# First attention input loaded in both orders, its statistics spread by products of ones with diagonals, keys and queries in one pass

## The chip, the core and the metric

The kernel runs on one core of one Trainium2 chip. The metric is device time of one execution in microseconds (us). Engine names are those of the profile: PE (TensorE matmul), PEld (its weight load), DVE (VectorE), ACT (ScalarE), POOL (GpSimd), SP (SyncE, which issues the DMAs).

## The reference, cut to what matters

Two sequences of 1024 tokens with 1024 features go through attention A (32 heads, rotary positions, causal, with ten adapter rows), a mixture feed-forward, attention B, and the feed-forward again, each behind a layernorm and with a residual. Only the entrance of stage A matters here, and only for the first sequence:

```
def _layernorm(x, axis=-1, eps=1e-05):
    m = jnp.mean(x, axis=axis, keepdims=True)
    v = jnp.var(x, axis=axis, keepdims=True)
    return (x - m) / jnp.sqrt(v + eps)
...
qkv = jnp.einsum('btc,oc->bto', x, w_attn)        # x is the normalized input
q, k, v = jnp.split(qkv, 3, axis=-1)
q = _apply_rope(q, cos, sin)
k = _apply_rope(k, cos, sin)
...
ak, av = (adapter rows through the k and v parts of w_attn)
```

All tensors are fp32. The tensor engine contracts over partitions, so the products for q, k and v need the normalized x with features on partitions (xnT), while x as it lies in memory has tokens on partitions, where mean and deviation of a token are found.

## The kernel before, in words

Tokens come in 8 tiles of 128 (t = 0 to 7), features in 8 blocks of 128 (c), tokens also in two halves of 512 (n). Heads are made in groups of four (g = 0 to 7): one group's keys and queries are 128 rows each, a group of values is made two at a time. The attention of group 0 starts as soon as its first half is there, and runs while later groups are projected.

*Order.* The order on PE, POOL and SP is that of the program text. On DVE and ACT a scheduler orders the instructions when the kernel is built; the built order is fixed, and each engine takes its instructions in that order. The projections are Python generators that a `Filler` steps between the rounds of the attention (`attend`, L478), by a budget of estimated nanoseconds; its `chores` (L64 to L70) are small DVE, POOL or DMA steps, one issued at each step of the generators, and `flush` issues what is left of one kind.

*Entrance before (L1089 to L1105).* SP loads four x tiles (`x_load`, tag "pr"), the adapter rows adT, the key and query weights of group 0 (`qk_load`), the value weights (`v_load`), then four further x tiles among cos, sin and gate. `layernorm` (L242) does for each tile two bn_stats and one bn_aggr on DVE (L247, L251), a few 128x1 operations on DVE and ACT (L254 to L267), and the normalization of 128x1024 on DVE (L271). `half` (L758) turns four tiles by PE transposes (`transposed`, L285, 32 of 128x128 for a half), whose banks DVE and ACT copy in turn into xnT (L233, L235). The first half is turned before the projection, the second (passed as `between`) inside it.

*First projection (`project_first`, L958).* For each half: eight k products of 512 columns (kp), then eight q products (qp), one bank each, then the values (`values_first`, L1044, vp, four tiles of 128 tokens). `rotate` (L915) applies the rotary positions to a finished bank: DVE shuffles (L920) and multiplies by cos (L921), POOL multiplies by sin and adds (L924, L925). Between k and q of the first half stands `adapter_keys` (L902): a small product akp and the DVE product aks (L905). `adapter_parts` (L892) makes the adapter rows' keys (ap_k) and values (ap_v, L897), `adapter_values` (L908) makes avp on PE and avs on DVE (L912). Between the halves stand `between`, then `begin(0, 1)`, which makes ap_k of group 1, and `combine(0)`, which queues chores.

*Banks.* PSUM has one bank under the tag "ps" (`bank`, L161), used in turn by ownT, ap_k, akp, ap_v, the adapter scores (as), avp and the next ap_k; a pair ca, cb (`next_bank`, L167) for the projections; two double banks for the scores sc; and one for y. A product into a bank waits until the last reader of what was there is done.

*Splitting.* `mm` (L196) issues a product either whole or as four products of 32 columns of the weights; `flip`, a transpose, switches to whole, the attention's rounds switch to split.

*SBUF.* The "tt" ring has five 128x512 buffers; "mo" two of 128x1024; "h16" two, which hold xnT of the two halves.

Of the kernel before, what the change touches and what calls it, by code (L numbers as in the profile page):

```python
# [14 lines left out]
F32 = mybir.dt.float32  # L15
# [133 lines left out]
def tile_model(ctx: ExitStack, tc: tile.TileContext, d, out: bass.AP):  # L149
# [17 lines left out]
    def next_bank(shape, name):  # L167
        pair.rotate(1)
        return block_bank(shape, name, 1)
# [424 lines left out]
    def stage_a(wk, big):  # L594
        ca = wk
        identb = of["identb"] = ca.tile([P, P], BF16, tag="identb", name="identb", bufs=1)
        dve.tensor_copy(identb, ident)
# [27 lines left out]
        dve.tensor_reduce(tosum[:, 0, :], ones_at, AX.X, ALU.add)  # L625
        for h in range(1, 4):
            pool.tensor_copy(tosum[:, h, :], tosum[:, 0, :])
# [130 lines left out]
        def half(b, n, xns):  # L758

            xnT[b, n] = big.tile([P, NC, HF], F32, tag="h16", name=f"xnT{b}_{n}")  # L760
            for i in range(4):
                yield from transposed(xns[4 * n + i], xnT[b, n][:, :, i * P : (i + 1) * P], f"a{b}_{4 * n + i}", by=(next_bank, next_bank))

        def moments_ahead():
# [26 lines left out]
            def load(c):  # L791
                for k in (c, c + 4):
                    x = big.tile([P, T], F32, tag="t4k", name=f"xc{k}")
                    sp.dma_start(x, d["x1T"][k * P : (k + 1) * P, :])
                    at.append(x)
# [139 lines left out]
        def project(b, g, between=None):  # L935
# [9 lines left out]
            if b == g == 0:  # L945
                yield from project_first(between)
            else:
                yield from project_blocks(b, g)
# [9 lines left out]
        def project_first(between):  # L958
            wqk = wqk_at[0, 0]
            yield adapter_parts("k0", lambda c: wqk[:, c, 1, :], P)  # L960
            for n in range(2):
                if n == 1:
                    yield from between
                    yield from begin(0, 1)
                    combine(0)
                xh = xnT[0, n]
                for s, key in ((1, "k"), (0, "q")):
                    qp = next_bank([P, HF], f"{key}p0_{n}")
                    for c in range(NC):
                        mm(qp, lhsT=wqk[:, c, s, :], rhs=xh[:, c, :], start=(c == 0), stop=(c == NC - 1))  # L970
                        yield HF * COL
                    rotate(0, 0, key, n, qp)
                    if n == 0 and key == "k":
                        yield adapter_keys(0)
                yield ("qk", 0, 0, n)
                yield from values_first(n)
            combine_first(0)
# [66 lines left out]
        def values_first(n):  # L1044
# [5 lines left out]
            for t in range(0, 4, 2):  # L1050
# [7 lines left out]
                if n == 0 and t == 2:  # L1058
                    yield adapter_values(0)
            if n == 1:  # L1060
                wv_at[0, 2] = v_load(0, 2)
# [29 lines left out]
        wqk_at[0, 0] = qk_load(0, 0)  # L1091
        wv_at[0, 0] = v_load(0, 0)
        xns = []
        for t in range(NT):
            if t + 4 < NT:
                xs.append(x_load(0, t + 4, wk, "pr"))
            xns.append(layernorm(big if t < 3 else wk, "t4k" if t < 3 else "pt", xs[t], f"a0_{t}"))
            if t == 0:
                sp.dma_start(cos, d["cos"])
                sp.dma_start(sin, d["sin"])  # L1100
                sp.dma_start(gate, d["gating"].partition_broadcast(P))
                tp = bank([NH, P], "ownT")
                flip(tp, own.rearrange("p h j -> p (h j)"), ident)
                dve.tensor_copy(ownT, tp)
        fill.add(half(0, 0, xns))  # L1105
        ahead = moments_ahead()
        for b in range(B):
            for g in range(NG):

                old = b * NG + g - 3  # L1110
                fill.add(project(b, g, half(0, 1, xns) if b == g == 0 else None),
# [715 lines left out]
```

## Time and profile before

| | |
|---|---|
| median of 3 runs | 2320.02 us (2316.45 to 2323.06) |
| the profiled execution | 2318.73 us |
| its span, first to last instruction | 2316.9 us |
| mean granted PE clock | 0.996 |
| PE busy | 2272.1 us, 98% |
| DVE, ACT, POOL busy | 62%, 47%, 26% |
| k products of the first half start | 19.44 us |
| first scores (sc) start | 38.67 us |
| k products of the second half start | 57.81 us |

The profile shows one execution. The chain of waits follows the work that ended last back from the end: at each step to what released it, or to the instruction before it on its engine; its start times differ by some hundredths from those of the timeline, because it counts from the release. The timeline merges like instructions that follow each other: start, length, engine, line, operation, output and inputs, count, and in brackets the idle time before them with what ended it. Stages give each engine's busy time, the granted clock and the DMA's share and rate in a stretch of the span. A fp32 product of 512 columns is two PE instructions, each 592 ns long and 430 ns after the one before it.

### The profile page before, as it was taken

The page shows a single profiled execution, that of the slowest core. Times are in us where ns is not written, and L with a number is a line of the kernel's source. Part 1 is how long each engine was busy: PE and PEld are TensorE (multiplying, and loading weights), DVE is VectorE, ACT ScalarE, POOL GpSimd, SP SyncE. Part 2 cuts the span into 40 slices and gives each one's busy share as a digit, 9 for nine tenths or more (in the row PEclk, how much of TensorE's full clock was granted, in tenths as well). Part 3 has the DMA queues.
Part 4 walks back from the last instruction along what each step waited for, and adds up shares of the span by engine and source line. Part 5 has one row for each costly group of instructions (what it writes and reads, how often), then busy time and mean ns, then how long its engine had stood idle before and what let it go on. Part 6 is the DMA issues. An engine that isn't in the chain of part 4 may idle for free.

```text
span 2316.9 us, 61351 instructions
## 1 busy us (share of the span) xinstructions
PE 2272.1 (98%) x25246; PEld 1039.5 (45%) x25246; DVE 1445.3 (62%) x4394; ACT 1087.4 (47%) x2084; POOL 613.7 (26%) x957
## 2 busy tenths in 40 slices
PE   8999999999999999999999999999999999999999
PEld 4425443454444544345433445575433553233454
DVE  6686677776656666666752246567766765675453
ACT  3356665666656666566652001012455546665100
POOL 1432234343322223222212124202111111122422
PEclk9999999999999999999999999999999999999999
DMA  5443434644433333333322674542323202323553
GB/s 177 157 131 101 126 108 141 195 128 153 150 95 106 94 112 92 102 105 95 109 71 91 207 245 160 163 156 77 114 93 104 99 18 84 110 83 119 181 161 122
DMA packets 188473, 285.78 MB, mean 123 GB/s; under 512 B 20112, under 2 KB 85792, under 8 KB 188192
## 3 DMA queue, kind: packets, MB, share of 16 engines
q1 hardware_dynamic: 188192, 281.86, 37.9%
q8 instruction: 198, 3.24, 0.6%
q14 instruction: 83, 0.68, 0.1%
HBM read 223.58 MB, written 55.58 MB: 120 GB/s over the span
## 4 chain that ended last, share of the span: by engine, by line
PE 88%; DVE 7%; DMA 2%; ACT 1%; issue 1%; POOL 0%; SPq 0%; DVEq 0%; POOLq 0%; ACTq 0%
PE st L415 10%; PE sc L343 7%; PE y L201 6%; PE y_A L437 6%; PE y_f L199 5%; PE x L201 4%; PE z L201 4%; PE z_f L199 4%; PE st L413 3%; PE y_v L201 3%; PE x_f L199 3%; PE y_B L437 2%; PE y_f L201 2%; PE y_p L199 2%; PE z_v L201 2%; PE hp_f L199 2%
## 5 line engine op out<-in xcount | busy, mean ns | idle before, releaser
L549 ACT ACTIVATE pt<-st 128x1024 f32<-128x1024 f32 (+1 forms) x418 | 423.9, 1019 | 541.4 <-PE st L415 422.3
L364 ACT ACTIVATE pr_A<-pr_A,nmax_A 128x896 f32<-128x896 f32 (+7 forms) x512 | 390.1, 766 | 54.2 <-DVE nmax_A L356 53.4
L356 DVE CUSTOM_DVE_ANT_0 pr_A<-sc,mask 128x512 f32<-128x512 f32 (+3 forms) x512 | 250.0, 535 | 173.1 <-PE st L415 88.6
L343 PE MATMUL sc<-kT,qT 32*128 32x512 f32 (+3 forms) x1536 | 317.2, 522 | 3.4 <-POOL qT L925 2.1
L415 PE MATMUL st<-qT,kT 32*128 32x512 f32 (+3 forms) x1536 | 296.2, 486 | 0.0
L356 DVE CUSTOM_DVE_ANT_0 pr_A<-sc,mask,part_A 128x512 f32<-128x512 f32 (+1 forms) x256 | 156.2, 647 | 123.7 <-PE sc L343 76.3
L422 POOL TENSOR_SCALAR_AFFINE_SELECT pt<-pt 128x256 f32<-128x256 f32 x256 | 102.5, 418 | 429.5 <-ACT pt L549 427.1
L240 POOL TENSOR_TENSOR xf<-xf,b_base 128x256 f32<-128x256 f32 x100 | 75.2, 782 | 406.8 <-DVE xn_f L271 283.4
L364 ACT ACTIVATE pr_B<-pr_B,nmax_B 128x1024 f32<-128x1024 f32 x128 | 145.5, 1141 | 33.0 <-DVE nmax_B L356 32.9
L437 PE MATMUL y_A<-pt,v 128*32 128x512 f32 (+3 forms) x1536 | 157.5, 496 | 0.0
L343 PE MATMUL sc<-kq,qk 32*128 32x512 f32 x512 | 135.8, 650 | 3.4 <-DVE nmax_B L356 2.4
L415 PE MATMUL st<-rows_B,kq 32*128 32x512 f32 x512 | 135.9, 647 | 1.2 <-ACT pt L549 1.0
L415 PEld LDWEIGHTS st<-qT,kT 32*128 32x128 f32 x1536 | 129.0, 185 | 14.9 <-issue 10.7
L413 PE MATMUL st<-rows_A,ones 3*128 3x512 bf16 (+3 forms) x768 | 123.2, 329 | 6.4 <-DVE nmax_A L356 4.1
L356 DVE CUSTOM_DVE_ANT_0 pr_B<-sc,zeros,part_B 128x512 f32<-128x512 f32 x128 | 91.0, 747 | 54.6 <-PE sc L343 54.5
L413 PEld LDWEIGHTS <-ones 3*128 3x128 bf16 x768 | 36.2, 91 | 190.0 <-issue 184.0
L924 POOL TENSOR_TENSOR qr<-qr,sin 128x256 f32<-128x256 f32 x64 | 61.6, 962 | 206.7 <-DVE qr L920 201.3
L201 PE MATMUL y<-tt,wqk 128*32 128x512 f32 x960 | 116.1, 594 | 0.0
L356 DVE CUSTOM_DVE_ANT_0 pr_B<-sc,zeros 128x512 f32<-128x512 f32 x128 | 83.5, 686 | 51.7 <-PE sc L343 51.6
L343 PEld LDWEIGHTS sc<-kT,qT 32*128 32x128 f32 x1536 | 109.4, 183 | 11.8 <-POOL qT L925 3.2
L201 PE MATMUL x<-xnT,wqk 128*32 128x512 f32 x936 | 114.0, 600 | 0.0
L364 ACT ACTIVATION_READ_ACCUMULATOR pr_A<-pr_A,nmax_A 128x1 f32 x512 | 97.2, 190 | 0.0
(406 smaller groups left out, 4072.3 us busy)
## 6 DMA issues: line engine op xcount, KB each, us to landing
tt<-td SPq DMA_DIRECT2D x264, 256.0 KB
qkb_f<-tf SPq DMA_DIRECT2D x96, 256.0 KB
qkb_s<-tf SPq DMA_DIRECT2D x84, 256.0 KB
wqk<-in_w_attnT SPq DMA_DIRECT2D x32, 512.0 KB
xf<-x SPq DMA_DIRECT2D x25, 512.0 KB
xa<-in_x SPq DMA_DIRECT2D x16, 512.0 KB
wv<-in_w_attnT SPq DMA_DIRECT2D x8, 1024.0 KB
yd<-ys SPq DMA_DIRECT2D x32, 256.0 KB
```

Of the source, the lines that this page charges most:

```text
L199: return pe.matmul(out, lhsT=lhsT, rhs=rhs, start=start, stop=stop, skip_group_check=True)
L201: pe.matmul(out[i : i + 32], lhsT=lhsT[:, i : i + 32], rhs=rhs, start=start, stop=stop, skip_group_check=True)
L240: pool.tensor_add(dst[:, i : i + 2 * P], a[:, i : i + 2 * P], b[:, i : i + 2 * P])
L343: yield w * COL, lambda: pe.matmul(dst[:, o : o + w], lhsT=self.qt[rows, qc : qc + P], rhs=self.kt[rows, c0 : c0 + w], start=True, stop=True)
L356: minimum[0] = dve.tensor_tensor_reduce(pr[:, c0 : c0 + w], sc[:, i, o : o + w], m, -self.scale, BIG if c0 == 0 else self.part[:, col], AL ...
L364: tc.keep_in_program_order(act.activation(pr[:, :nk], pr[:, :nk], AF.Exp, bias=self.nmax[:, col], scale=-1.0, accum_out=self.sums[:, col]))
L413: yield w * COL / 4, lambda: pe.matmul(dst[:, o : o + w], lhsT=of["ones"][three, :], rhs=self.rows[three, off : off + w], start=True, stop ...
L415: yield w * COL, lambda: pe.matmul(dst[:, o : o + w], lhsT=self.kt[rows, kb * P : (kb + 1) * P], rhs=rhs, start=self.extra, stop=True)
L422: pool.affine_select(out=dg, in_=dg, compare_op=ALU.is_ge, fill=0.0, base=0, pattern=[[0, 2], [1, P]], channel_multiplier=-1)
L437: pe.matmul(self.y[32 * h : 32 * h + 32, off : off + w], lhsT=self.value(h, kb), rhs=pt[h // 2][:, h % 2, o : o + w], start=self.opens, st ...
L549: act.activation(pt[:, :, low_:wide_], st[:, :, low_:wide_], AF.Exp, scale=ts[0][0].scale)
L924: pool.tensor_mul(qr[:, hs], qr[:, hs], sin[:, cols][:, hs])
```

## The change

The host passes the first input also with axes exchanged (xT, for both sequences; before, only the second sequence had it, as x1T). The kernel then loads xT of sequence 0 straight into xnT, in four DMAs of 1 MB, and normalizes it in place. `half` and with it all 64 transposes and their 16 copies go, and so does the 128x1024 normalization of each tile.

Mean and deviation are needed along the columns, in every partition. `moments_first` makes the statistics of four tiles (x tiles are still loaded for that) and two 128x512 tiles that hold, for each of four token tiles, a diagonal of the means or of the reciprocal deviations. `spread_first` multiplies these by a matrix of ones on PE, four products of 128 columns for each, and ACT copies the bank into a `spread` tile. `normalize_first` subtracts and multiplies block by block: eight subtractions and five multiplications on DVE, three multiplications on POOL in two pieces each.

For the first half all of this stands ahead of the projection. For the second half the statistics are issued after the first half's normalization; the spreads are issued on PE inside the first half's values, and the normalization becomes chores under the key "xn".

In `project_first` the first half's k and q products alternate block by block, into two banks; `adapter_keys` comes after both. In the second half k comes before q, as before. SP loads xT, cos and sin ahead of the value weights, and the four later x tiles after those. Some small steps (identb, tosum, ownT) move behind the first half.

```diff
-        def half(b, n, xns):
-            xnT[b, n] = big.tile([P, NC, HF], F32, tag="h16", name=f"xnT{b}_{n}")
+        def moments_first(n, xs):
+            mv = wk.tile([P, 4, 2], F32, tag="mv0", name=f"mv0_{n}", bufs=1)
             for i in range(4):
-                yield from transposed(xns[4 * n + i], xnT[b, n][:, :, i * P : (i + 1) * P], ...)
+                stats = wk.tile([P, 2, 6], F32, tag="stats", name=f"stats0_{4 * n + i}", bufs=2)
+                for h in range(2):
+                    dve.bn_stats(stats[:, h, :], xs[i][:, h * HF : (h + 1) * HF])
+                dve.bn_aggr(mv[:, i], stats)
+            ve, r, e = (wk.tile([P, 4], F32, tag=tag, name=f"{tag}_{n}", bufs=1) for tag in ("ve0", "rs0", "es0"))
+            dve.tensor_scalar(ve, mv[:, :, 1], EPS, None, ALU.add)
+            act.activation(e, ve, AF.Ln)
+            act.activation(r, e, AF.Exp, scale=-0.5)
+            dve.tensor_mul(e, r, r)
+            dve.tensor_mul(e, e, ve)
+            dve.tensor_scalar(e, e, -0.5, 1.5, ALU.mult, ALU.add)
+            dve.tensor_mul(r, r, e)
+            diagonals = []
+            for i, column in enumerate((mv[:, :, 0], r)):
+                dg = big.tile([P, 4, P], F32, tag="tt", name=f"dg{i}_{n}")
+                dve.tensor_mul(dg, ident[:, None, :].to_broadcast([P, 4, P]), column[:, :, None].to_broadcast([P, 4, P]))
+                diagonals.append(dg)
+            return diagonals
+        def spread_first(n, diagonals):
+            for i, dg in enumerate(diagonals):
+                pb = next_bank([P, 4, P], f"spread{i}_{n}")
+                for t in range(4):
+                    mm(pb[:, t, :], lhsT=all_ones[:, :P], rhs=dg[:, t, :], start=True, stop=True)
+                act.copy(spread[i][:, n * HF : (n + 1) * HF], pb.rearrange("p t c -> p (t c)"))
+        def normalize_first(n):
+            cols = slice(n * HF, (n + 1) * HF)
+            for c in range(NC):
+                x = xnT[0, n][:, c, :]
+                yield lambda x=x: dve.tensor_sub(x, x, spread[0][:, cols])
+                if c % 2 and c > 1:
+                    yield lambda x=x: in_pieces(pool.tensor_mul)(x, x, spread[1][:, cols])
+                else:
+                    yield lambda x=x: dve.tensor_mul(x, x, spread[1][:, cols])
...
                 if n == 1:
-                    yield from between
                     yield from begin(0, 1)
+                    fill.flush("xn")
                     combine(0)
                 xh = xnT[0, n]
-                for s, key in ((1, "k"), (0, "q")):
-                    qp = next_bank([P, HF], f"{key}p0_{n}")
-                    for c in range(NC):
-                        mm(qp, lhsT=wqk[:, c, s, :], rhs=xh[:, c, :], start=(c == 0), stop=(c == NC - 1))
-                        yield HF * COL
-                    rotate(0, 0, key, n, qp)
-                    if n == 0 and key == "k":
-                        yield adapter_keys(0)
+                steps = [(key, s, c) for c in range(NC) for s, key in ((1, "k"), (0, "q"))]
+                if n:
+                    steps.sort(key=lambda step: -step[1])
+                qp = {}
+                for key, s, c in steps:
+                    if c == 0:
+                        qp[key] = next_bank([P, HF], f"{key}p0_{n}")
+                    mm(qp[key], lhsT=wqk[:, c, s, :], rhs=xh[:, c, :], start=(c == 0), stop=(c == NC - 1))
+                    yield HF * COL
+                    if c == NC - 1:
+                        rotate(0, 0, key, n, qp[key])
+                if n == 0:
+                    yield adapter_keys(0)
...
                 if n == 0 and t == 2:
                     yield adapter_values(0)
+                if n == t == 0:
+                    spread_first(1, diagonals)
+                    yield 8 * P * COL
+                    for op in normalize_first(1):
+                        fill.chore("xn", op)
...
         wqk_at[0, 0] = qk_load(0, 0)
+        for n in range(2):
+            xnT[0, n] = big.tile([P, NC, HF], F32, tag="h16", name=f"xnT0_{n}")
+        def xt_load(n):
+            for i in range(2):
+                sp.dma_start(xnT[0, n][:, 4 * i : 4 * i + 4, :],
+                             d["xT"][0, 4 * i * P : (4 * i + 4) * P, n * HF : (n + 1) * HF].rearrange("(c p) t -> p c t", p=P))
+        xt_load(0)
+        sp.dma_start(cos, d["cos"])
+        sp.dma_start(sin, d["sin"])
         wv_at[0, 0] = v_load(0, 0)
-        xns = []
-        for t in range(NT):
-            if t + 4 < NT:
-                xs.append(x_load(0, t + 4, wk, "pr"))
-            xns.append(layernorm(big if t < 3 else wk, "t4k" if t < 3 else "pt", xs[t], f"a0_{t}"))
...
-        fill.add(half(0, 0, xns))
+        sp.dma_start(gate, d["gating"].partition_broadcast(P))
+        later = [x_load(0, t, wk, "pr") for t in range(4, NT)]
+        xt_load(1)
+        all_ones = big.tile([P, HF], F32, tag="tt", name="all_ones")
+        pool.memset(all_ones, 1.0)
+        spread = [big.tile([P, T], F32, tag="mo", name=f"spread{i}") for i in range(2)]
+        spread_first(0, moments_first(0, xs))
+        for op in normalize_first(0):
+            op()
+        diagonals = moments_first(1, later)
+        dve.tensor_copy(identb, ident)
+        dve.tensor_reduce(tosum[:, 0, :], ones_at, AX.X, ALU.add)
...
+        tp = bank([NH, P], "ownT")
+        flip(tp, own.rearrange("p h j -> p (h j)"), ident)
+        dve.tensor_copy(ownT, tp)
...
-        "x1T": a[A + "x"][1].T,
+        "xT": np.swapaxes(a[A + "x"], 1, 2),
```

In the built program of the changed kernel the scheduler put, on DVE, the first three pairs of bn_stats of the second half's tiles ahead of the k shuffle, the fourth pair and the mean diagonal between the k shuffle and aks, and avs behind the whole second normalization and three of the steps that `begin(0, 1)` and `combine(0)` queue (s, tn, s).

## The prediction

> **What bounds the kernel now.** I read the page first, then the chain of waits over the first 150 us, then the timeline, the stages and single tiles there.
>
> ```profile
> PE 2272.1 (98%) x25246; PEld 1039.5 (45%) x25246; DVE 1445.3 (62%) x4394; ACT 1087.4 (47%) x2084; POOL 613.7 (26%) x957
> PE   8999999999999999999999999999999999999999
> ```
>
> TensorE (PE) is busy for 98% of the span; only the first slice stands out. So a microsecond taken from PE's work or its idle time in the opening is a microsecond of the kernel, and one added there is never won back, because what follows has no slack. By the order of the built program, the changed kernel issues on PE exactly the same sequence from the scores that follow the values of the second half on; all differences lie in the first 77 us of the trace of before. The chain there:
>
> ```profile
> 14.09 0.83 DVE xn_a L271
> 15.05 1.94 PE xt_a L205 x8
> ...
> 19.51 7.06 PE kp L199 x16
> 26.72 6.94 PE qp L199 x16
> 33.66 1.00 PE ap_v L897 x16
> 34.66 4.08 PE vp L199 x18
> 38.74 1.08 PE sc L343 x16
> ...
> 51.41 0.56 PE avp L910 x2
> 51.96 0.60 PE xt_a L205 x4
> ...
> 57.30 0.57 PE ap_k L897 x16
> 57.88 7.06 PE kp L199 x16
> ```
>
> (Columns: start, length, what.) From 19.51 on it is PE all the way: keys, queries, adapter values (ap_v), values (vp), first scores (sc), and from 51.96 to 57.30 the transposes of the second half, 5.3 us in which PE mostly waits for copies.
>
> **Step 1, the first products.** Now kp starts at 19.51, behind eight normalized-and-transposed pieces. In the changed kernel DVE makes four statistics without the 0.8 us normalizations (L271): a pair of bn_stats is 1.29, with its bn_aggr a pitch of 1.45, so from 4.59 (first x landed), with the two small copies moved in between, the fourth ends at 10.7. Mean diagonal (no row; the nearest is a 128x512 subtraction, L225, 0.69; bounds 0.64 of L921 and 1.10 of L228 beside POOL) ends at 11.6; four small operations and the second diagonal at 13.1. Each spread is four products, that is 8 PE instructions; 8 transposes took 1.94 at this point, so PE ends at 13.5 and 15.5; ScalarE copies at 0.59 (L235) end at 14.2 and 16.2. The ownT copy stands before the subtractions on DVE and ends at 16.2. Two subtractions and a multiplication at 0.65 give column block 0 at 18.1. Gain **1.4**; if the diagonals or spreads take their bounds, 0.2 to 2.5.
>
> Is xT there? Up to its first half 4.33 MB, to its second 5.38 MB must land. The stages of before moved 1.06, 2.61, 4.20 and 6.17 MB up to 5, 10, 15 and 20 us, so they land at about 15.3 and 18.0; wanted at 16.2 and 20.7. At the slowest full stage (311 GB/s) it is 18.9 for the second: still in time. The 4.2 MB more of DMA are hidden here; the four later x tiles end at 9.57 MB, 29.6 us (32.4 at 311 GB/s), when the statistics that want them wait for PE anyway. DVE's 13 and POOL's 3 normalizing steps run ahead of PE (1.76 per block of k and q).
>
> **Step 2, the cold clock.**
>
> ```profile
> L205 PE MATMUL xt_a<-ident,xn_a x32: 421/421/473, 9.5 to 18.5; 128*128 128x128 f32 x32
> ```
> ```profile
> L205 PE MATMUL xt_a<-ident,xn_a x32: 272/273/331, 51.9 to 57.0; 128*128 128x128 f32 x32
> ```
> ```profile
> 128.00:130.00 2.00, 1.02 (x16) 0.31 (x8) 1.97 (x5) 0.00 (x0) 1.85 (x3) 1.00 0.80 232
> 130.00:131.00 1.00, 0.00 (x0) 0.00 (x0) 0.47 (x1) 0.00 (x0) 0.99 (x1) 1.00 1.16 340
> 131.00:132.00 1.00, 0.89 (x8) 0.31 (x8) 0.00 (x0) 0.00 (x0) 0.92 (x3) 0.77 1.13 273
> 132.00:133.00 1.00, 1.00 (x8) 0.20 (x8) 0.58 (x5) 0.25 (x1) 1.00 (x2) 0.50 0.20 47
> ```
>
> The same transpose takes 421 ns before 18.9 us and 273 later: PE starts slow, and four solid microseconds of transposes ended that just ahead of kp (592 ns each from its first). The second pair of rows (busy PE, PEld, DVE, ACT, POOL; clock; DMA) shows the way back: PE did little from 128.3 to 131.1 and then had a clock of 0.50, for 3.4 us by the stages after it, costing half of that, 1.7. In the changed kernel only spreads, ownT and ap_k, with gaps, run ahead of kp, so I let kp run cold for 3.4 us: **+1.7**, bounds 0 and 3.4.
>
> The Trainium skill, TensorE: Matmul & The Clock Gate, "Part 4: PE-mode transpose", says that transposes do not count as busy and never release the clock. The trace differs: after nothing but transposes kp ran at full rate. By the page, before would have started kp cold too, step 2 would be 0 and the sum 1.7 smaller; I follow the rows.
>
> **Step 3, first new wait.** Now the key bank is finished 7 us before the query bank, and its rotation and the small aks product (L905) hide under qp. Made together, both end together, 14.0 us after the start; the last k product 0.9 earlier. PE's next instruction but one, ap_v (L897), writes the one "ps" bank that aks is read from: it must wait for DVE's aks. And on DVE, in the built order, stand between the wait for kp and aks:
>
> ```profile
> 26.62 0.73 DVE L920 STREAM_SHUFFLE kr<-kp 128x512 f32<-128x512 f32 x1
> ...
> 29.70 0.64 DVE L921 TENSOR_TENSOR kT<-kp,cos 128x512 f32<-128x512 f32 x1
> ...
> 30.37 0.19 DVE L905 TENSOR_TENSOR aks<-akp,own 128x40 f32<-128x40 f32 x1
> ```
>
> shuffle 0.73, bn_aggr 0.20, two bn_stats 1.29 (the eighth tile, stuck behind the shuffle although its data is there), kT 0.65, bn_aggr 0.20, q shuffle 0.73, ve 0.15, diagonal 0.69, es 0.26, qT 0.67, es 0.20, aks 0.19: 5.96; neighbours overlap by some 0.05, so 5.4. That is 4.6 after the end of qp. PE then does ap_v 1.00 and vp 4.08 and reaches the scores 9.7 after qp; before it was 38.74 - 33.66 = 5.1. **+4.6** (bounds 3.8; 5.6 if two of these take 1.10 beside POOL). POOL's rotation ends some 2.5 earlier than sc needs it, so it is not late next; parts_v, one bn_stats and all first softmax rows queue behind, and shift with it.
>
> PE stands 4.3 us, longer than at 128, so the clock falls: 1.7 if it is cold for 3.4 from the restart, up to 3.4 if for two such stretches. **+2.3**, bounds 0 and 3.4.
>
> **Step 4, second new wait.** Take S for the start of sc (38.74 now). ap_k of the second half starts at S+18.56 now. Without transposes PE goes: sc 1.08, 40 vp 2.30, as 0.30, 16 vp 0.86, first spread 0.86 (8 x 0.107), S+5.4. The second spread wants the bank that ACT's copy of v frees; that copy ended at 44.93 now, S+6.2, behind eight exponentials. Then 0.86, sc 1.07, 128 vp 7.05 (120 took 6.61), avp 0.56: S+15.8, 2.8 earlier than now. But ap_k takes the "ps" bank that avs (L912) reads on DVE, and DVE meets avs only behind the whole second normalization: from the first spread copy, S+6.85, 13 steps of 0.65 (8.45), four 512-wide row minima at 0.62 to 0.69 (2.6), two transposes 0.50, s, tn and s at 0.69 (2.07), avs 0.60: 14.2, S+21.1. In before avs ran at 52.0 on an idle DVE. POOL multiplies three blocks at the same time, and DVE steps beside POOL took 1.10 in places: bounds 14.2 and 20 (all 13 steps); I add 0.5. So ap_k at S+21.6, **+3.0** against S+18.56 (bounds 2.5 and 8). PE stands 5.8 us; cold clock again **+2.3** (0 to 3.4). The normalization itself is then done, and kp runs through; in the tile-split form 8 products still take 6.9 (x, L201: 16 in 1.72, two products).
>
> **Sum**: -1.4 + 1.7 + 4.6 + 2.3 + 3.0 + 2.3 = **+12.5 us**. The profiled execution took 2318.73 (span 2316.9 and 1.8 around it); it is 1.3 below the median 2320.02, well inside the runs shown. Forecast 2331.2.
>
> **Rivals.**
> (a) *The clock does not follow.* Only the waits count: -1.4 + 4.6 + 3.0 = +6.2, 2325. For it: PE has scattered work near each wait. Against it: rows 130 to 133. Chance 0.12.
> (b) *The waits stay covered* (not slower). If aks and avs come before PE wants them, there remain the start, -1.4, and the transposes, 15.8 against 18.56, -2.8: -4.2, 2314.5, and 2312 with the start at its better bound and the second spread not waiting for v. It decides where DVE has aks within 0.3 us of the end of qp and avs by S+15.8: DVE would have to be 4.3 and 5.8 us shorter, which no row gives. Against it also is that DVE takes its instructions as they stand in all these rows. Chance 0.11, half of it beyond 0.3%.
> (c) *DVE slower than sized*: most of the 13 steps beside POOL at 1.10 and both cold stretches double: 5 + 2.2 more, 2339 and beyond. Chance 0.05.
>
> The forecast, 0.72, spans 2325 (all lesser bounds) to 2339. 0.3% is 7 us, about what a measurement of this kernel can tell from no change. Beyond +7 lie 0.66 of the forecast, 0.04 of (a), all of (c): 0.75 slower. Within: 0.06, 0.08 and 0.05: 0.19. Faster: 0.06. The range leaves out (b) and most of (c): 2320 to 2340.
>
> **What would show it.** kp starts near 18 and is slow at first; after akp PE idles some 4 us, released by DVE's aks; after avp it idles 5 to 6, released by avs; the granted clock is 0.5 after each; the k products of half two start near 68 instead of 57.9. I am wrong if PE runs through either place, if the clock stays at 1.00, or if something behind 130 us gives time back, which the unchanged PE order speaks against.

## The result, and the profile after

The changed kernel took 2335.31 us (median of 4 runs, 2334.21 to 2339.84) against 2320.68 us of the kernel before beside it (4 runs, 2316.45 to 2323.06): ratio 1.0072, 95% interval 1.0057 to 1.0087. It is slower by 14.6 us; the forecast was 12.5 us slower. The profiled execution took 2334.21 us, 15.5 more than that of before.

The page of the changed kernel, to be held against the two lines shown of before:

```profile
PE 2268.8 (97%) x25424; PEld 1032.8 (44%) x25424; DVE 1453.9 (62%) x4386; ACT 1082.9 (46%) x2068; POOL 629.6 (27%) x970
PE   6899999999999999999999999999999999999999
```

PE has 3.3 us *less* to do (2268.8 against 2272.1), and the span is 15.6 longer: the loss is idle time, and it shows in the first two of the 40 slices, which fell from 8 to 6 and from 9 to 8 tenths. The chain of waits there:

```profile
33.96 0.72 DVE kr L952 x2
...
34.77 1.15 DVE stats L760 x2
...
37.41 0.59 DVE dg L773
...
39.40 0.12 DVE aks L937
...
39.56 1.94 PE ap_v L929 x16
41.50 4.82 PE vp L199 x18
46.32 1.09 PE sc L343 x16
...
61.76 0.57 PE avp L942 x2
62.33 7.17 issue
69.50 1.08 PE ap_k L929 x16
70.58 8.47 PE kp L201 x64
```

In before this stretch was PE from 19.51 on. Now the chain leaves PE twice. From 33.96 to 39.52 it runs over DVE: the rotation of k, statistics of the eighth tile (L760), a diagonal (L773), aks; only then ap_v goes. From 62.33 to 69.50 the chain says "issue": it saw no releaser, but avs (L944) ends at 69.4 on DVE. The stages give a clock of 0.50 from 19.1 to 22.5, from 39.6 to 43.0 and from 66.9 to 73.7 us (1.00 between), so ap_v takes 1.94 (1.00 before), vp 4.82 (4.08), kp 8.47 (7.06).

The scores of the second half start 14.1 us later than before (90.60 against 76.49 by the timeline). The first of ACT's large exponentials (L549) starts at 97.3 us in before and 14.14 us later here; the shift stays within 0.04 of that up to 383 us, but for one exponential (13.87, at 161). Beyond, it moves between 14.0 and 18.0, and the span ends 15.6 later.

### The profile page after: what moved, and what is told of

Read it like the earlier page. It is cut to its first block, busy times and chain, and to the rows that moved or that the text cites. A ratio compares the mean times of both kernels' runs of the same rounds, so it can differ in the third digit from the quotient of the medians.

```text
span 2332.5 us, 61703 instructions
## 1 busy us (share of the span) xinstructions
PE 2268.8 (97%) x25424; PEld 1032.8 (44%) x25424; DVE 1453.9 (62%) x4386; ACT 1082.9 (46%) x2068; POOL 629.6 (27%) x970
## 4 chain that ended last, share of the span: by engine, by line
PE 86%; DVE 7%; DMA 2%; issue 2%; ACT 1%; POOL 0%; SPq 0%; DVEq 0%; POOLq 0%; ACTq 0%
PE st L415 9%; PE sc L343 7%; PE y L201 6%; PE y_A L437 6%; PE y_f L199 5%; PE x L201 4%; PE z L201 4%; PE z_f L199 4%; PE st L413 3%; PE y_v L201 3%; PE x_f L199 3%; PE y_B L437 2%; PE y_f L201 2%; PE y_p L199 2%; PE z_v L201 2%; PE hp_f L199 2%
## 5 line engine op out<-in xcount | busy, mean ns | idle before, releaser
L549 ACT ACTIVATE pt<-st 128x1024 f32<-128x1024 f32 (+1 forms) x418 | 423.4, 1018 | 542.7 <-PE st L415 425.9
L201 PE MATMUL y<-tt,wqk 128*32 128x512 f32 x960 | 116.3, 594 | 0.2
L201 PE MATMUL x<-xnT,wqk 128*32 128x512 f32 x936 | 113.7, 599 | 0.0
```

Of the source, the lines that this page charges most:

```text
L201: pe.matmul(out[i : i + 32], lhsT=lhsT[:, i : i + 32], rhs=rhs, start=start, stop=stop, skip_group_check=True)
L549: act.activation(pt[:, :, low_:wide_], st[:, :, low_:wide_], AF.Exp, scale=ts[0][0].scale)
```

## Experiments

What a whole run shows is uncertain by some us; the trace shows to hundredths where the loss arises, though in one execution. So the table gives for each kernel, from the timeline, the starts of ap_v, of the second half's keys and of its scores (where these stop in between, their second part too), and the **shift**: how much later than in before the first L549 starts. The whole times stand behind. Up to 0.9 us of a shift is no effect of an edit: in the kernels with the changed entrance the first spread starts between 11.37 and 12.29 us, although nothing ahead of it was edited, because the x tiles land at different times (DVE waits 0 to 0.64 us for the third).

| kernel | ap_v | keys 2 | scores 2 | shift | median us (runs) | ratio to before (95%) |
|---|---|---|---|---|---|---|
| before | 33.59 | 57.81 | 76.49 | 0 | | |
| the change | 39.56 | 70.32 | 90.60 | +14.14 | 2335.31 (4) | 1.0072 (1.0057 to 1.0087) |
| e1_keys_early | 36.35 | 68.36 | 88.07 | +11.59 | 2330.24 (7) | 1.0039 (1.0020 to 1.0058) |
| e2_avs_early | 39.12 | 62.56 | 83.32 | +6.88 | 2328.29 (9) | 1.0035 (1.0022 to 1.0049) |
| e3_both_early | 35.26 | 60.47 | 79.07, 82.39 | +7.11 | 2326.43 (10) | 1.0029 (1.0015 to 1.0042) |
| e4_warm | 39.47 | 68.23 | 86.85, 89.30 | +14.02 | 2340.46 (4) | 1.0088 (1.0061 to 1.0115) |
| e5_all_dve | 37.31 | 65.27 | 85.03 | +8.58 | 2324.03 (1) | |
| e6_together_alone | 33.00 | 57.89 | 76.57 | +0.08 | 2320.83 (10) | 1.0005 (0.9995 to 1.0015) |
| e7_other_bank | 35.77 | 59.88 | 78.48, 82.29 | +5.37 | 2323.75 (10) | 1.0010 (1.0001 to 1.0019) |
| e8_all_early | 33.25 | 55.38 | 73.98 | -2.51 | 2317.00 (12) | 0.9981 (0.9972 to 0.9991) |
| e9_second_half | 35.84 | 58.59 | 81.05, 82.14 | +5.22 | 2326.24 (12) | 1.0019 (1.0008 to 1.0031) |
| e10_best | 41.44 | 62.59 | 81.19 | +4.70 | 2324.52 (12) | 1.0025 (1.0012 to 1.0038) |
| e11_late_spread | 32.49 | 55.70 | 74.29, 77.63 | +3.66 | 2322.99 (1) | |
| e12_own_bank | 31.28 | 55.86 | 74.46 | -2.03 | 2316.39 (12) | 0.9992 (0.9980 to 1.0003) |

### Are the two waits what the forecast said they are?

**e1_keys_early** moves akp and aks ahead of the fifth pair of products:

```diff
+                    if n == 0 and (key, c) == ("q", 3):
+                        yield adapter_keys(0)
-                if n == 0:
-                    yield adapter_keys(0)
```

> The changed kernel, but the adapter's keys (akp and aks) are yielded after the query's product of c=3 instead of after the whole loop, so that aks stands on DVE ahead of the rotations and of the eighth tile's moments. Theory (a wait on the bank that aks releases): the 4.65 us in which PE stands before ap_v go, and with them the slow stretch at 39.6 to 43.0; the first scores start at about 41.0 to 42.0 us instead of 46.3 (the second half of qT leaves POOL at 42.8 and then binds). The wait before the second ap_k, for avs behind the second normalization, stays at 5 to 8 us, so the second half's scores start at 84 to 87 us instead of 90.7. Rival (the wait is for something else, the rotations on POOL or the statistics): ap_v still starts at about 39.5 and nothing moves. Time: 2329 to 2332 by the theory, 2335 by the rival.

The 4.65 us went; ap_v followed qp at once. But only 2.55 us of shift were gained. One loss lies ahead of the place of the move: here the start ran at full clock, and the product of c = 3 stood 1.86 us for POOL's xnT. It started 7.28 us after the first kp, exactly as in the change (there slow products had filled the time, and 0.17 was left to wait); but the clock then fell to 0.50, from 26.2 to 29.6. The other loss came up behind the wait removed: PE stood 0.79 us for kT and 1.43 before the second part of the first scores:

```profile
25.44 1.34 PE L199 MATMUL kp<-xnT,wqk 128*128 128x512 f32 x2 [1.86 <-POOL xnT L221]
...
44.52 0.93 PE L343 MATMUL sc<-kT,qT 32*128 32x384 f32 x8 [1.43 <-POOL qT L957]
```

The theory of the wait holds; my price for what is next was too low by some 3 us (the last part of the scores starts at 44.5, where I had expected the first at 41 to 42). The second wait stayed at 7.18.

**e2_avs_early** moves avp and avs ahead of the second spread:

```diff
-                if n == 0 and t == 2:
-                    yield adapter_values(0)
                 if n == t == 0:
+                    yield adapter_values(0)
                     spread_first(1, diagonals)
```

> The changed kernel, but the adapter's values (avp and avs) are yielded at the first v tile of the first half instead of at the third, ahead of the second half's spread and normalization on DVE. Theory (the second ap_k waits for the bank that avs releases, behind the second normalization): PE's 7.2 us before the second ap_k go, and the slow stretch from 66.9 to 73.7 with them; keys of the second half start at 62.5 to 64 us instead of 70.6 and the second half's scores at 81 to 84 instead of 90.7. The first wait (4.65 us) stays. Rival (the normalization itself is what the keys wait for, so that avs only stands at its end by chance): the idle time moves to the second half's kp and stays over 4 us in sum. Time: 2326 to 2329 by the theory, 2331 to 2335 by the rival.

As the theory said: ap_k ran at 62.12, keys at 62.56, scores at 83.32. Stops of 1.14 us (ACT's copy of the spread) and 1.96 (xnT from POOL, c = 3) took the place of 7.2, 3.1 in sum, less than the rival's 4.

**e3_both_early** makes both edits.

> The changed kernel with both moves of the two experiments above: adapter's keys after the query's c=3, adapter's values at the first v tile. Theory: both waits go and both slow stretches; keys of the second half at 57 to 60 us (before 57.9, after 70.6), the second half's scores at 76 to 79 (before 76.6, after 90.7). The two waits with the cold stretches are then the whole loss, and the earlier start of the products is worth about 1 us: 2318 to 2323. Rival (the change costs besides, by 13 slower steps on DVE and POOL or by the cold clock at the start): second half's scores stay over 80 us, time 2325 or more.

The rival won here. Both waits and both slow stretches behind them went, and yet the shift is +7.11, no better than e2 alone. The second half's scores broke in two, 2.61 us idle for POOL's qT, and the clock fell after that. Removing the waits alone does not bring the kernel back.

**e7_other_bank** moves nothing. It only gives akp and avp of group 0 a bank that is unused so early:

```diff
+        def y_bank(shape, name):
+            return ps.tile(shape, F32, tag="y", name=name, bufs=1)
...
-            akp = (block_bank if g else bank)([P, NH], f"akp{g}")
+            akp = (block_bank if g else y_bank)([P, NH], f"akp{g}")
...
-            avp = (block_bank if g else bank)([NH, 2 * P], f"avp{g}")
+            avp = (block_bank if g else y_bank)([NH, 2 * P], f"avp{g}")
```

> The changed kernel with one edit: akp and avp of the first pair of heads go to the bank of the attention outputs, which nothing uses so early, so that ap_v and the second ap_k no longer share a bank with them. No step is moved. Theory (both waits are for the bank alone): ap_v follows akp at 35 us instead of 39.6 and the second ap_k follows avp; PE then waits for the rotation on DVE before vp (under 1.5 us) and for POOL's qT before the first scores, which start at 41 to 43 us instead of 46.3; keys of the second half at 59 to 61 instead of 70.6, its scores at 78 to 83 instead of 90.7; time 2323 to 2328. Rival (the waits are for the data that stands behind aks and avs): the idle time appears one instruction later and the second half's scores stay at 87 or later.

Lines of its PE timeline:

```profile
35.77 1.07 PE L932 MATMUL ap_v<-wv,adT 128*32 128x256 f32 x16
37.48 4.15 PE L199 MATMUL vp<-wv,xnT 128*128 128x256 f32 x18 [0.65 <-DVE kT L956]
59.42 0.65 PE L932 MATMUL ap_k<-wqk,adT 128*32 128x128 f32 x16
82.29 0.71 PE L343 MATMUL sc<-kT,qT 32*128 32x256 f32 x8 [3.10 <-POOL qT L960]
```

Neither ap_v nor ap_k has a bracket: both waits were for the one shared bank and for nothing else, and without them the shift falls by 8.8 us (0.8 of it is this execution's earlier start: first spread at 11.41 against 12.22). That is the proof of the mechanism. What is left, +5.37, is mostly POOL: its rotation is late (the last line, and 1.51 before the first scores), and its part of the first normalization makes PE stand 1.86 us at c = 3, with a fall of the clock behind it.

### Does the clock fall because PE stands still?

**e4_warm** fills the two waits with products that the reference does not have, into the unused bank:

```diff
+        def warm(xh, count):
+            wy = ps.tile([P, HF], F32, tag="y", name=f"warm{count}", bufs=1)
+            for i in range(count):
+                pe.matmul(wy, lhsT=wqk_at[0, 0][:, 0, 0, :], rhs=xh[:, 0, :], start=True, stop=True, ...)
...
+                    warm(xnT[0, 0], 8)
                     yield from begin(0, 1)
...
                     yield adapter_keys(0)
+                    warm(xh, 5)
```

> The changed kernel with products added that the reference does not have, into a bank that nothing reads: 5 of 128x512 after akp and 8 ahead of the second ap_k, which fill PE's two waits (at 0.88 us each 4.4 and 7.1 us). The waits themselves stay. Theory (the clock falls because PE stands still): the slow stretches at 39.6 and 66.9 go, ap_v takes 1.0 us instead of 1.94, the second half's kp 7.1 us instead of 8.5, and the second half's scores start at 86.5 to 88.5 us instead of 90.7; time 2330 to 2333. Rival (the slow stretches have another cause, or the clock's loss is made up by later waits): starts at 90 to 91 us and 2335.

Lines of its PE timeline:

```profile
39.47 1.07 PE L929 MATMUL ap_v<-wv,adT 128*32 128x256 f32 x16 [0.29 <-DVE aks L937]
89.30 0.83 PE L343 MATMUL sc<-kT,qT 32*128 32x256 f32 x8 [1.73 <-POOL qT L957]
90.06 3.45 PE L201 MATMUL vp<-wv,xnT 128*32 128x256 f32 x32
```

The stages of the change (first two rows) and of e4 (last row; busy PE, PEld, DVE, ACT, POOL, then clock and DMA):

```profile
39.60:42.90 3.30, 3.30 (x20) 1.77 (x21) 2.79 (x5) 0.00 (x0) 3.06 (x4) 0.50 0.69 281
66.90:73.60 6.70, 4.10 (x32) 1.77 (x36) 5.40 (x9) 0.27 (x1) 3.01 (x3) 0.50 0.21 78
...
39.60:42.90 3.30, 3.30 (x27) 2.46 (x24) 2.60 (x5) 0.00 (x0) 2.96 (x4) 1.00 0.72 288
```

From 66.9 to 73.6 e4 has 1.00 too. ap_v starts where it did and takes 1.07; the second half's kp takes 7.08; the scores start 3.75 us earlier than in the change (1.7 and 2.1, as read from the longer rows). So the clock's theory holds and rival (a) of the forecast falls. But the gain is soon gone: POOL's qT holds the second part of the scores 1.73 us, and the clock then halves the products behind them (3.45 for what takes 1.93). The shift is +14.02. So taking the two cold stretches away gained nothing: close behind them stood another wait, on a chain over DVE and POOL. The whole time is above the change's, with intervals that overlap; the trace puts this later (shift 17 from 500 to 1650 us, 22 from 1940 on); most of the last step is one more fall of the clock (see the end).

### Where did the forecast's missing 2 us of the second wait come from?

**e5_all_dve** takes POOL out of the normalization (`if c % 2 and c > 1:` becomes `if False:`).

> The changed kernel with the multiplications of c = 3, 5 and 7 on DVE too, none on POOL. Theory (DVE's steps take 1.2 us instead of 0.65 because POOL works on the same data beside them, which is the term that the forecast sized at 0.5 us): the second normalization's 16 steps take about 0.65 us each although DVE has 3 more, avs ends at 66 to 67.5 us instead of 69.4, the wait before the second ap_k is 5 to 6 us instead of 7.2, and the second half's scores start at 88 to 89 us instead of 90.7. Rival (the 1.2 us are the operation's own price at that place): three steps more on DVE, avs 2 to 3.5 us later, scores at 92 to 94.

DVE's timeline in the second normalization, first of the change, then of e5:

```profile
59.60 2.42 DVE L790 TENSOR_TENSOR xnT<-xnT,spread 128x512 f32<-128x512 f32 x3
61.94 1.21 DVE L794 TENSOR_TENSOR xnT<-xnT,spread 128x512 f32<-128x512 f32 x1
63.08 2.34 DVE L790 TENSOR_TENSOR xnT<-xnT,spread 128x512 f32<-128x512 f32 x2
```

```profile
57.13 1.28 DVE L790 TENSOR_TENSOR xnT<-xnT,spread 128x512 f32<-128x512 f32 x2
58.33 1.28 DVE L794 TENSOR_TENSOR xnT<-xnT,spread 128x512 f32<-128x512 f32 x2
59.53 1.28 DVE L790 TENSOR_TENSOR xnT<-xnT,spread 128x512 f32<-128x512 f32 x2
```

A step beside POOL takes 1.21, alone it follows the one before after 0.60. The last line of either fence is not the last step. From its first subtraction to its last multiplication DVE needs 13.0 us for 13 steps in the change (53.02 to 66.02) and 12.7 for 16 steps in e5 (50.56 to 63.83, less 0.6 for s). The three multiplications that POOL was given saved DVE nothing. Idle time before the second ap_k fell to 4.59, below the window of the first theory (5 to 6), where the rival wanted it longer. More was gained than expected, 5.6 us of shift, because the first half gained as well: no product waited for POOL and the clock stayed up, so qp ended at 32.3 instead of 34.6.

There the same conflict is worse, on POOL's side. POOL's timeline of the change from 20.5 to 22 us:

```profile
20.53 4.65 POOL L221 TENSOR_TENSOR xnT<-xnT,spread 128x256 f32<-128x256 f32 x1 [15.49 <-DVE xnT L790]
```

One piece of 128x256, 0.73 alone, takes 4.65: it ends at 25.2, just after DVE's gapless string of normalizing steps (to 24.6). That is why c = 3 is there only at 25.9. The Trainium skill, SBUF — State Buffer, "Who interferes with whom", says that a DVE instruction with two SBUF inputs and a GpSimd instruction that reads SBUF contend for a shared port pair, and that the second one blocks fully until the first is done. These rows fit that: beyond the time alone, 0.5 to 0.6 for DVE's step and 3.9 for POOL's piece, which ends 0.6 after the string, about its length alone. That POOL's piece waited through six DVE steps, and not for one, the page does not say.

### The parts alone

**e6_together_alone** is the kernel before with only k and q of the first half alternating, akp behind both, and the other bank of e7.

> One part of the change alone, in the kernel before: the first half's products of k and q alternate, and akp comes after both, with akp and avp in the other bank so that no wait on aks is added. Layernorm and transposes stay as before. Theory (keys and queries that end together bring both rotations at once, behind ap_v on DVE and one after the other on POOL): PE waits under 1 us for kT and 1 to 2 us for POOL's qT, the first scores end at 42 to 43.5 us (before 39.8), and what is lost stays: the second half's scores start at 78.5 to 80.5 us (before 76.6); time 2322 to 2325. Rival (the order costs nothing by itself, only the shared bank made it wait): the first scores end at 39.5 to 40.5, the second half's start at 76 to 77, time 2319 to 2321.

The rival won: shift +0.08. POOL made PE wait 0.39 us. In this execution the first x landed 0.53 us earlier than in before (4.06 against 4.59) and kp started 0.52 earlier, so the order itself costs some 0.6 us. So "keys and queries together" costs little by itself; it costs more where DVE's rotation steps stand behind statistics and diagonals, which this kernel does not have there, and through the shared bank.

**e9_second_half** is the kernel before with the second half alone by spread products (statistics on DVE behind the copies of the first half's transposes, avp ahead of the spread, the other bank).

> One part of the change alone, in the kernel before: the first half is normalized and transposed as before, k then q; only the second half's x comes with axes exchanged and is normalized by spread products, with akp and avp in the other bank and avp ahead of the spread. Theory (the second half's 32 transposes, 5.4 us of PE, become 2.0 us of products, and the loss of the change sits in the first half's order and the two waits): first scores at 38.5 to 39.5 us as before, keys of the second half at 54 to 57 (before 57.9), its scores at 73 to 76 (before 76.6): 1 to 3.4 us gained, 2316 to 2320. Rival (the second normalization, 16 steps on DVE and POOL after the first scores, is too slow for the keys even so): keys of the second half wait over 3 us in sum for xnT, scores at 77 or later.

Neither theory fits. The new order on DVE put the first copy out of the transposes at 15.99 us instead of 13.11, so the first keys started 2.24 us late, which is not a cost of the spread products. Behind that, PE waited 1.34 us for ACT's copy of the spread and 1.96 for POOL's xnT, and the clock fell. It shows that the second half's part, too, needs its place on DVE; what it would give there this kernel does not tell.

### Can the change be made to pay?

**e11_late_spread** is e7 with another order of the first half's products, k four steps ahead of q (akp follows k) and POOL's blocks (3, 5, 7) late:

```diff
-                steps = [(key, s, c) for c in range(NC) for s, key in ((1, "k"), (0, "q"))]
-                if n:
-                    steps.sort(key=lambda step: -step[1])
+                if n == 0:
+                    order = "k0 q0 k1 q1 k2 q2 k4 q4 k6 k3 k5 k7 q6 q3 q5 q7".split()
+                else:
+                    order = [key + str(c) for key in "kq" for c in range(NC)]
+                steps = [(o[0], int(o[0] == "k"), int(o[1])) for o in order]
```

> The changed kernel with akp and avp in the other bank and the first half's products in the order in which k ends four steps before q; the second spread and its normalization stay where the change has them, after the first v pair. It tells apart the two further edits of the experiment with everything early (second half's scores at 74.0 to 75.1 us there, 78.5 to 83.0 with the other bank alone). Theory (the order frees the first rotations, and the place of the spread frees the second normalization): first scores at 38 to 39.5 us without waits for POOL, and the second half's scores complete at 77 to 81 us, because POOL's qT or xnT is late there. Rival (all of it is the order): complete at 74.5 to 76.

ap_v came at 32.49, 3.3 us before that of e7, but the first scores still waited 1.50 for POOL's qT (expected: no wait) and the second half's 2.62; those were complete as late as the theory said (from 77.63). **e8_all_early** adds the place of the second spread: behind the first v tile instead of the second, so that DVE normalizes where it stood idle before the first scores (4.8 us in the change), and avp after the first v pair. The second half's products follow the blocks' order 0, 1, 2, 4, 6, 3, 5, 7.

```diff
                         yield 256 * COL
+                    if n == t == i == 0:
+                        spread_first(1, diagonals, (bank, y_bank))
+                        yield 8 * P * COL
+                        for op in normalize_first(1):
+                            fill.chore("xn", op)
...
-                if n == 0 and t == 2:
+                if n == t == 0:
                     yield adapter_values(0)
-                if n == t == 0:
-                    spread_first(1, diagonals)
-                    yield 8 * P * COL
-                    for op in normalize_first(1):
-                        fill.chore("xn", op)
```

> The changed kernel with four edits: akp and avp in the other bank; the first half's products in the order k0 q0 k1 q1 k2 q2 k4 q4 k6 k3 k5 k7 q6 q3 q5 q7, so that k ends four steps before q and its rotation runs beside them; the second spread after the first v tile instead of the second, so that the normalization runs in DVE's idle time before the scores; avp at the end of the first v pair. Theory (beyond the two waits, the loss left in the experiment with both moves is the rotations of k and q that come at once, and the late normalization): first scores at 39 to 42 us without waits for POOL, keys of the second half at 54 to 57 us (before 57.9), its scores at 73 to 77 (before 76.6); time 2316 to 2321. Rival (the rest of the loss sits in the start, up to the end of the first q, which this does not touch): scores of the second half at 78 or later, time 2322 or more.

Lines of its PE timeline:

```profile
39.88 1.16 PE L199 MATMUL spread<-dg,all_ones 128*128 128x128 f32 x8 [0.73 <-DVE dg L773]
40.97 1.15 PE L343 MATMUL sc<-kT,qT 32*128 32x128 f32 x16
73.98 1.15 PE L343 MATMUL sc<-kT,qT 32*128 32x256 f32 x16
```

No bracket on either line of scores: POOL is in time, and with it the transposes saved come through. The shift is -2.51, the ratio 0.9981 (0.9972 to 0.9991): 4.4 us faster than the kernel before, the first version that gains. From e7 the order gave 1.7 us of shift, and the place of the spread, with those of avp and of the second half's blocks, 6.2; the three were not tried apart.

**e10_best** adds three edits: all multiplications on DVE (blocks in order again), the first xT transfers in four pieces, and the second half's statistics issued after the first rotation of k, those of the last two tiles tied behind it:

```diff
-            for i in range(2):
-                sp.dma_start(xnT[0, n][:, 4 * i : 4 * i + 4, :],
+            k = 4 if n else 2
+            for i in range(0, NC, k):
+                sp.dma_start(xnT[0, n][:, i : i + k, :],
...
+                    if n and i > 1:
+                        tc.add_manual_dep(r.ins, shuffled[0].name, ..., reason="behind the keys")
```

> The kernel of the experiment with everything early, with three more edits: all multiplications of the normalization on DVE, the first half of x with axes exchanged in four transfers of two c each instead of two of four, and the statistics of the seventh and eighth tile behind the first rotation of k. Theory (the start is set by the landing of the first transfer, and DVE's steps are faster without POOL beside them): the first kp starts at 17.0 to 18.0 us instead of 18.5, the second half's scores start at 72 to 73.5 us instead of 74.0; time 2315 to 2317. Rival (the start is set by the spread products and their copies on ACT, and the slow steps were covered): no more than 0.3 us of difference anywhere, 2317.

The line of its PE timeline that decides:

```profile
24.84 1.08 PE L938 MATMUL ap_k<-wqk,adT 128*32 128x128 f32 x16 [9.31 <-DVE ownT L1177]
```

Both theories missed. In this kernel the scheduler put the copy of ownT behind the whole first normalization on DVE (it ends at 24.8), and ap_k wants the bank that this copy reads: the forecast's two waits a third time, made by me. **e12_own_bank** gives ownT the other bank:

```diff
-        tp = bank([NH, P], "ownT")
+        tp = y_bank([NH, P], "ownT")
```

> The kernel of the last experiment with one edit: ownT goes to the other bank too, so that the first ap_k no longer waits for its copy behind the first normalization (9.3 us there). Theory (a third wait of the same kind, on the one shared bank, was all that made that kernel slower): ap_k follows the copy of ownT's bank no more, the first kp starts at 16.9 to 17.9 us (25.9 there, 18.5 in the experiment with everything early), the second half's scores at 72 to 73.5 us (81.2 there, 74.0), 2314.5 to 2317. Rival (the four small transfers land no earlier, or PE waits for DVE's normalization instead): kp starts at 18.4 or later or stops between its steps, scores of the second half at 74 or later, 2317 or more.

Lines of its PE timeline:

```profile
17.13 1.12 PE L199 MATMUL kp<-xnT,wqk 128*128 128x512 f32 x2 [0.77 <-DVE xnT L800]
39.25 2.07 PE L199 MATMUL spread<-dg,all_ones 128*128 128x128 f32 x8 [1.12 <-DVE dg L779]
```

The first keys started at 17.13 as the theory said (xT landed at 15.2, against 16.6 in the change, and the copy of ownT no longer stands ahead of the normalization), and qp ended 2 us earlier than in e8. But the diagonals did not come earlier by as much (the second started at 38.50, in e8 at 39.14, the first later), so PE stood 1.00 and 1.12 us before the two spreads, the clock fell, and all was given back: scores at 74.46, which is the rival's window. Against before it is 0.9992 (0.9980 to 1.0003), no difference shown.

## Why the prediction was right, by its own steps

| step | forecast | measured | |
|---|---|---|---|
| 1, first products | -1.4 | -0.8 (kp 18.64 against 19.44) | too good by 0.6 |
| 2, cold clock at the start | +1.7 | +2.1 (c = 3 started 7.28 us after the first kp, not 5.25) | near, but by another cause |
| 3, wait for aks | +4.6 | +4.65 | right |
| 3, clock | +2.3 | +1.6 | inside its bounds |
| 4, wait for avs | +3.0 | +4.7 (ap_k at S+23.25, not S+21.6) | mis-sized |
| 4, clock | +2.3 | +1.8 | inside its bounds |
| sum | +12.5 | +14.1 at the scores, +14.6 by the medians | |

The steps' misses (+0.6, +0.4, -0.7, +1.7, -0.5) partly cancel, so the sum is closer than the steps. The forecast's ends are mis-added: its own lesser bounds give 2322.5, not 2325, and the greater ones 2342, not 2339; the result lies inside either.

*Step 1* failed at "they land at about 15.3": the first xT landed at 16.6. The forecast counted bytes; the transfer was issued only at 9.22, because SP was busy for 5.74 us with the issue of the two wqk transfers ahead of it (5.47 already in before). That held DVE for 0.38 us; the rest of the 0.6 are tenths on the way. e12, where the first pieces are smaller, landed at 15.2 and started at 17.13.

*Step 2* is near in size, but its cause does not carry the cost. The product of c = 3 started 7.28 us after the first kp in the change and likewise in e1, e2, e3, e4 and e7; in e5, at full clock and without POOL, it was 5.25. In e1 and e7 the products ahead of it ran at full clock, and PE stood 1.86 us for POOL's xnT instead. So POOL's first piece (4.65 us, below e5) set the time, and the cold clock only filled it. The step that failed is "DVE's 13 and POOL's 3 normalizing steps run ahead of PE", which put this wait at nothing. Without POOL, in e5, PE ran through and qp ended 2.3 us earlier (0.1 of it by its start). The clock itself was a matter of phase. It was released at 15.66 by the spread products, which the forecast did not expect, and fell for one stretch at 19.07. In e5, e8, e11 and e12 the same start ran at full clock, in e1 and e7 the fall came at 26.2.

*Step 3* held to the tenth in its wait; e7 shows that the bank is the whole cause.

*Step 4* has the right mechanism and the mis-sized term "I add 0.5" for POOL. The first subtraction came at S+6.7 (forecast S+6.85). From there to the end of avs it took 16.4 us instead of 14.7 (14.2 and the 0.5). By e5, beside POOL 13 steps take as long as 16 alone: with 2.9 us of row minima and transposes taken off, 0.78 against 0.61 a step, 2.2 us in sum; s and tn at 1.21 instead of 0.68 are another 1.1; steps alone were shorter than sized (0.60 against 0.65). The bound of 20 stood in the text; the value taken lay too near its other end.

*What the forecast's sum hid.* By e4 the two clock terms (3.75 us of earlier scores there) were not additive: without them the rotation on POOL binds. "POOL's rotation ... is not late next" was true only behind the longer waits of step 3.

*Rival (b)*, waits covered, was priced at 2314.5. e7 is that case: shift +5.4, not -4.2. What its price left out are waits for POOL, 1.86 for xnT with 1.7 of clock behind it, 1.51 and 3.10 for qT, and 0.65 for DVE's kT, 8.8 in sum. Its -4.2 is not far from what e8 reaches (-2.5) once these are gone.

## What to carry to other kernels

When a change moves work on an engine that is 60% busy, list for every bank the reader that frees it and what now stands ahead of that reader in its engine's order: here two small DVE steps behind strings of others took back more than 64 transposes' removal gave, and another bank won some 8 us of it back. Behind each wait removed, ask at once for the next one: e7 removed 11.8 us of waits, and with them two falls of the clock, and gained some 8. Handing steps to a second engine that reads the same memory is no saving until a row shows both running side by side at the speed they have alone.

## What the runs showed of the hardware that was not expected

In the opening the clock falls after much shorter idle times than the 4.3 and 5.8 us that the forecast counted with, if these fall into one stretch. Its changes lie 3.41 us apart, or multiples of that. In the change it fell after the stretch from 15.66 to 19.07, in which PE stood for two gaps of 0.38 and 1.63 us; in e12 after gaps of 1.00 and 1.12; in e7 after one of 1.86. In e5 a gap of 1.40 at the same place as in the change left it at 1.00, and so did the 3.10 us in e7 before the second half's scores: counted in steps of 3.41 from its rise at 29.67, a boundary at 80.87 splits them into 1.68 and 1.42. No threshold is shown: later in the change the clock fell at 1992.0 after a stretch in which PE was busy for 79%, and stayed up through one, to 435.5, with 44%. The Trainium skill, TensorE: Matmul & The Clock Gate, "HAM oscillation — how this bites in real kernels", gives as its rule no idle gaps above some 3.4 us; these rows show that a gap little over half that is enough, and that one near it may not be. "What's actually happening" on the same page says that the window of 3413 ns runs freely, so that the point of change varies from run to run; that the same start is cold in some of these kernels and warm in others agrees with it.

Beyond 383 us a part of the shift's moves is the clock again: from 1787.0 to 1793.8 it was 0.50 in before, with 1.00 in the change (shift from 17.9 to 14.7), and from 1934.0 to 1937.4 0.50 in the change, with 1.00 in before (14.7 to 16.5). In e4 it was 0.50 from 1936.4 to 1943.2, which is 3.4 of the 4.8 us that its shift grew there (17.3 to 22.1). Another part is a wait of 1.90 us at 435 in the change, before a product (z_v, L201) for which before does not wait (14.2 to 16.4). What sets these off, and the smaller moves in e6 and e8, stay open.
